# LayerNorm output turned to features by VectorE blocks and SBUF transfers, for seven of eight chunks

## The chip, the cores and the metric

The kernel runs on one NeuronCore of a Trainium2 chip. The metric is the device time of one execution in microseconds. A core has a matrix engine (TensorE, PE in the profile; its weight loads are PEld), three element-wise engines (VectorE or DVE, ScalarE or ACT, GpSimd or POOL) and SyncE (SP), whose queue issues all of this kernel's DMAs. Each engine works through its own instructions in order and waits on semaphores.

## The reference

Two blocks follow each other on x of 2 batches x 2048 tokens x 512 features, all in float32. Cut to what matters:

```python
# block 1: a diagonal complex state space layer (S5) and a feed-forward, conditioned on t
y_mod = _ln(y) * (1 + scale_a) + shift_a
y = y + gate_a * _s5(y_mod, ...)            # a scan along the tokens
y_norm = _ln(y) * (1 + scale_c) + shift_c
y_mod = y_norm * (1 + scale_ff) + shift_ff
y = y + gate_ff * (gelu(y_mod @ W1 + b1) @ W2 + b2)
# block 2: attention, 16 heads of 32, between two conditioned norms
h = gamma * (_ln(hidden) * ln_g + ln_b) + beta
qkv = h @ Wqkv.T + bqkv
att = softmax(q @ k.T) / sqrt(D)
h1 = (att @ v) @ Wp.T + bp + hidden
return gamma * (_ln(h1) * ln_g + ln_b) + beta + h1
```

The scan and the recurrence need the tokens in their order. Attention does not: softmax and the sum over keys are the same for any order of the keys, as long as queries and outputs are put back in their rows.

## The kernel before

The tokens are cut into eight chunks of 512 (`CH`; four per batch), held as 4 tiles of 128 tokens (`TT`) by 512 features, with tokens on the partitions. Every matrix product needs its input the other way round: features on the partitions, as `fT` of 4 quarters (`KC`) of 128 features by 512 tokens. Three norms per chunk are turned like that: the one before S5, the one before the feed-forward and the one before attention.

`normalised` (L392) takes mean and deviation on VectorE and writes `xn`, of which there is one buffer. `features` (L403) then makes one quarter with `to_features` (L145): four TensorE transposes of 128x128 into one PSUM bank (L149), and one ScalarE activation that applies scale and shift and writes `fT` (L150). The banks come from `Banks` (L191): two that take turns, used by all the small products as well.

The loop over chunks (L628) is a schedule written out by hand. One pass does the feed-forward of chunk `now` in 16 steps f: `ff_first` (L484) multiplies by a column block of W1 into `ph` (2 buffers), ScalarE's Gelu makes `hid` (L491, 3 buffers), and `ff_second` (L495) multiplies the `hid` of the step before into `po` (L500). A table `due[f, half]` says which other work is put behind step f: half 0 after `ff_first(f)`, half 1 after `ff_second(f-1)`. In it stand, for the chunk behind, `at_norm` at (0, 1), the four quarters `at_features` from (2, 0) to (3, 1), the eight key and query products `at_heads` (L523) from (4, 1) on, and the four `at_values` from (12, 1) on; for the chunk ahead, `normalised` at (3, 1), the S5 quarters from (5, 0), S5 itself at 7 to 11, `ff_norm` at (12, 0) and the feed-forward quarters from (14, 0). `load_x` of the chunk after that is at (3, 1). Where the batch changes (the pass of chunk 3), `s5_gates` builds three gate rows on TensorE at (3, 0), a fourth row follows at (3, 1), and a fifth after that pass's feed-forward.

`at_norm` (L513) also adds a bias to x on POOL (L517) and stores x to the DRAM buffer `x2` (L518), from which the residual is read after attention. `at_heads` cuts its results into two halves and stores them to DRAM; `at_values` does the same whole. Attention (from about 1400 us) reads keys, queries and values back, block by block, and ends in `close` and `last_close`, which store rows of `out`.

The chunks' x tiles are three buffers in turn, `x0` to `x2`; `fT` has two buffers in turn by chunk, `f0` and `f1`, for S5 and the feed-forward, and one, `hT`, for attention. SP's queue holds the loads and stores in the order of the code.

Of the kernel before, what the change touches and what calls it, by code (L numbers as in the profile page):

```python
# [8 lines left out]
F32 = mybir.dt.float32  # L9
# [4 lines left out]
AF = mybir.ActivationFunctionType  # L14
# [5 lines left out]
P = 128  # L20
# [13 lines left out]
V_D, V_B1, V_B2, V_LNG, V_LNB, V_BQ, V_BK, V_BV, V_BP = 40, 44, 60, 64, 68, 72, 76, 80, 84  # L34
# [5 lines left out]
def tile_s5_block_then_sln_attention(  # L40
# [21 lines left out]
    nc = tc.nc  # L62
    NB, L, D = x.shape
    KC = D // P
    CH = 512
    TT = CH // P
# [12 lines left out]
    vec = const.tile([P, N_VECS], F32, name="vec")  # L79
# [22 lines left out]
    x2 = [dpool.tile([L, D], F32, name=f"x2_{b}") for b in range(NB)]  # L102
# [42 lines left out]
    def to_features(dst, xn, scale, shift, b, k, psum, tag):  # L145

        pt = psum.tile([P, CH], F32, name="pt_tf", tag=tag)
        for t in range(TT):
            nc.tensor.transpose(pt[:, t * P : (t + 1) * P], xn[:, t, k * P : (k + 1) * P], ident)  # L149
        nc.scalar.activation(  # L150
            dst[:, k, :], pt, AF.Identity,
            bias=shift[:, k, b : b + 1], scale=scale[:, k, b : b + 1],
        )
# [23 lines left out]
    xnp = late.enter_context(tc.tile_pool(name="xnp", bufs=1))  # L177
    xlate = late.enter_context(tc.tile_pool(name="xlate", bufs=1))
    wlate = late.enter_context(tc.tile_pool(name="wlate", bufs=1))
# [4 lines left out]
    xpool = early.enter_context(tc.tile_pool(name="xpool", bufs=1, side="right"))  # L184
# [3 lines left out]
    feat = early.enter_context(tc.tile_pool(name="feat", bufs=1, side="right"))  # L188
# [10 lines left out]

    order = [(b, c) for b in range(NB) for c in range(NCH)]  # L200
    index = {bc: i for i, bc in enumerate(order)}
    xt, xns, fts = {}, {}, {}

    def load_x(b, c):
        i = index[b, c] % 3
# [54 lines left out]
    for q in range(4):  # L260
        f = FC // 4
# [67 lines left out]
    t_re = s5c.tile([P, CH], F32, name="t_re")  # L329
    t_im = s5c.tile([P, CH], F32, name="t_im")  # L330
# [54 lines left out]
    gate, last, bus, hs, pos, hids = {}, {}, {}, {}, {}, {}  # L385
# [6 lines left out]
    def normalised(b, c):  # L392

        xc = xt[b, c]
        mean = small.tile([P, TT], F32, name="mean")
        rstd = small.tile([P, TT], F32, name="rstd")
        ln_stats(xc, TT, mean, rstd)
        xn = xnp.tile([P, TT, D], F32, name="xn")
        for t in range(TT):
            normalise(xn[:, t, :], xc[:, t, :], mean, rstd, t)  # L400
        xns[b, c] = xn

    def features(b, c, k, scale, shift, tag):  # L403
        if k == 0:
            fts[b, c] = (wlate if tag == "hT" else feat).tile([P, KC, CH], F32, name="fT", tag=tag)
        to_features(fts[b, c], xns[b, c], scale, shift, b, k, ones, None)

    def tag_of(b, c):
        return f"f{index[b, c] % 2}"
# [15 lines left out]
    def s5_turn(b, c):  # L425

        bu = bus.pop((b, c))
        m = [s5w.tile([P, CH], F32, name=f"m{i}") for i in range(6)]
        nc.vector.tensor_mul(m[0], bu[0], t_re)
        nc.vector.tensor_mul(m[3], bu[0], t_im)  # L430
        nc.vector.tensor_mul(m[1], bu[1], t_im)
        nc.vector.tensor_mul(m[2], bu[1], t_re)  # L432
        nc.vector.tensor_add(m[0], m[0], m[1])
        nc.gpsimd.tensor_tensor(m[2], m[2], m[3], ALU.subtract)  # L434
        bus[b, c] = m
# [48 lines left out]
    def ff_first(b, c, f):  # L484
        ph = ps1.tile([P, CH], F32, name="ph")
        for k in range(KC):
            nc.tensor.matmul(  # L487
                ph, w1_sb[:, k, f * P : (f + 1) * P], fts[b, c][:, k, :], start=k == 0, stop=k == KC - 1
            )
        hids[f] = work1.tile([P, CH], F32, name="hid", bufs=3)  # L490
        nc.scalar.activation(  # L491
            hids[f], ph, AF.Gelu_apprx_tanh, bias=vec[:, V_B1 + f : V_B1 + f + 1], scale=1.0
        )

    def ff_second(b, c, f):  # L495
# [9 lines left out]
    def ff_out(b, c):  # L505
        xc, po = xt[b, c], pos.pop((b, c))
        for t in range(TT):
            g = work1.tile([P, D], F32, name="gated")
            nc.vector.tensor_mul(g, po[:, t, :], gate[b, "gate_f"])  # L509
            nc.gpsimd.tensor_tensor(xc[:, t, :], xc[:, t, :], g, ALU.add)  # L510


    def at_norm(b, c):  # L513
        normalised(b, c)
        xc = xt.pop((b, c))
        for t in range(TT):
            nc.gpsimd.tensor_tensor(xc[:, t, :], xc[:, t, :], bp_row, ALU.add)  # L517
        nc.sync.dma_start(x2[b][c * CH : (c + 1) * CH, :].rearrange("(t p) d -> p t d", p=P), xc)  # L518

    def at_features(b, c, k):  # L520
        features(b, c, k, s_scale, s_shift, "hT")
# [38 lines left out]
    spare = ps1.tile([P, TT, D], F32, name="spare", tag="po", bufs=1)  # L560
# [67 lines left out]
    for i, now in enumerate(order):  # L628

        due = {(f, h): [] for f in range(FC + 1) for h in range(2)}  # L630
        ahead = order[i + 1] if i + 1 < len(order) else None
        behind = order[i - 1] if i else None

        def quarters_from(f, what, chunk):
            for k in range(KC):
                due[f + k // 2, k % 2].append((what, *chunk, k))

        if i == 0:
            due[1, 1].append((rest_of_mod,))
            due[2, 1].append((rows_of_biases,))  # L640
        if behind:
            due[0, 1].append((at_norm, *behind))
            quarters_from(2, at_features, behind)
            for j in range(2 * KC):
                due[4 + j, 1].append((at_heads, *behind, j))
            for t in range(TT):
                if ahead:
                    due[12 + t, 1].append((at_values, *behind, t))
        if ahead:
            if ahead[1] == 0:  # L650
                due[3, 0].append((s5_gates, ahead[0]))
                due[3, 1].append((gate_row, ahead[0], "gb2", gate_b2))
            due[3, 1].append((normalised, *ahead))
            quarters_from(5, s5_features, ahead)
            due[7, 1].append((s5_in, *ahead))
            due[7, 1].append((s5_turn, *ahead))
            due[8, 1].append((s5_scan, *ahead))
            due[8, 1].append((s5_direct, *ahead))
            quarters_from(10, s5_out, ahead)
            due[12, 0].append((ff_norm, *ahead))  # L660
            quarters_from(14, ff_features, ahead)
        if i + 2 < len(order):
            due[3, 1].append((load_x, *order[i + 2]))

        def run_due(at):
            for what, *args in due[at]:
                what(*args)

        for f in range(FC):
            ff_first(*now, f)  # L670
            run_due((f, 0))
            if f:
                ff_second(*now, f - 1)
            run_due((f, 1))
        ff_second(*now, FC - 1)
        ff_out(*now)
        if ahead and ahead[0] != now[0]:
            gate_row(ahead[0], "gate_f", mod[:, GATE_F])
    early.close()
# [190 lines left out]
    def invert(b, c, heads=slice(0, NH), width=64):  # L870
        sm = held.pop((b, c, "sm"))
        nc.vector.reciprocal(sm, sm)
        nc.sync.dma_start(invd[b][heads, c * CH : (c + 1) * CH].rearrange("h (s i) -> h s i", i=width), sm)

    def fetch(b, qt):

        at = slice(qt * P, (qt + 1) * P)
        o4 = work.tile([P, NG, P], F32, name="o4")
        nc.sync.dma_start(o4, od[b][:, at].rearrange("(g r) q -> r g q", r=P))
        by = work.tile([P, NG, P], F32, name="by")  # L880
        heads = invd[b][:, at].rearrange("(g j) q -> j g q", j=4)
        for j in range(4):
            nc.sync.dma_start(
                by[32 * j : 32 * j + 32, :, :], heads[j : j + 1, :, :].to_broadcast([32, NG, P])
            )
        xr = work.tile([P, D], F32, name="xr", bufs=3)
        nc.sync.dma_start(xr, x2[b][at, :])
        held[b, qt] = o4, by, xr
# [66 lines left out]
    def close(b, qt):  # L955

        h, ht, w, mv, y, v = held.pop((b, qt))
        nc.gpsimd.tensor_tensor(ht, w, ht, ALU.add)
        nc.sync.dma_start(out[b, qt * P : (qt + 1) * P, :], ht)


    def deviation(b, qt):
# [14 lines left out]
    def last_close(b, qt):  # L977
        h, y = held.pop((b, qt))
        nc.gpsimd.tensor_tensor(h, h, ending[b][1], ALU.add)
        nc.gpsimd.tensor_tensor(y, y, h, ALU.add)  # L980
        nc.sync.dma_start(out[b, qt * P : (qt + 1) * P, :], y)

# [128 lines left out]
    keeps, m = [], 0  # L1113
# [15 lines left out]
    due = {}  # L1129
# [21 lines left out]
    for b in range(NB):  # L1151
        for c in range(NQ):
            j = NP * (blocks.index((b, NPAIR - 1, c)) + 1) + 1
            if (b, c) == (LB, LC):
                most, rest = slice(0, NH - 4), slice(NH - 4, NH - 2)
                j = NP * (N - 1)
# [22 lines left out]
            for t in range(TT):  # L1179
                qt = c * TT + t  # L1180
                if b == LB:
                    k = j + 3 + 2 * t
# [8 lines left out]
                else:  # L1191

                    k = NP * (NPAIR * NQ * (b + 1) + 2 + 3 * qt // 2)
# [19 lines left out]
    for j in range(FIRST, NP * N + 2):  # L1213
# [18 lines left out]
        n, i = block_at(j + AHEAD)  # L1232
# [91 lines left out]
```

## Time and profile before

| What | Value |
|---|---|
| Time, median of 3 runs | 3458.43 us (3457.08 to 3461.29) |
| The profiled execution | 3459.56 us, span 3457.8 us, granted TensorE clock 0.990 |
| PE busy over the span | 3335.5 us, 96% |
| DVE, ACT, POOL busy | 2151.7, 1939.8, 2137.8 us |
| Chunk stage (to about 1450 us) | one regular pass 170 us |
| TensorE transposes of L149 | 384, of which 336 between 100 and 1400 us |

The chunk stage takes slices 1 to 17 of the profile's 40, attention the rest. A row of a group gives the line, the engine, the operation, what it writes and reads, how often, and after the bar the busy time in us, the mean of one in ns and the engine's idle time before it. A row of the timeline gives the start and the time taken, in us from the span's start, and in brackets the idle time ahead of it and what ended it. TensorE's instructions are pipelined, so one can start before the one ahead has ended: for its cost, take the distance from start to start. "x8" of a product is four matmuls, each in two instructions.

### The profile page before, as it was taken

Reading aid. Unit: us, or ns where it says so; the run is one execution under the profiler, and the core shown is the slowest. Engines: PE = TensorE matmul, PEld = TensorE weight load, DVE = VectorE, ACT = ScalarE, POOL = GpSimd, SP = SyncE. Lnnn points to the kernel's source line nnn. Section 1 sums busy time; section 2 is a strip of 40 time slices with the busy share of each in tenths; the row PEclk is TensorE's granted clock in tenths of the full one; section 3 lists DMA queues with packets and bytes.
Section 4 is the critical chain, followed back from the end, with each engine's and each line's share of the span. In section 5 each row is a group of like instructions: output and inputs, shape, how many; then the busy total and the mean of one; then the engine's idle time right before and its main releaser. Section 6 shows DMA issues by size and latency. Waiting matters only on the chain.

```text
span 3457.8 us, 34348 instructions
## 1 busy us (share of the span) xinstructions
PE 3335.5 (96%) x11764; PEld 1508.3 (44%) x11764; DVE 2151.7 (62%) x2976; ACT 1939.8 (56%) x2208; POOL 2137.8 (62%) x1162
## 2 busy tenths in 40 slices
PE   7999999999999999999999999999999999999997
PEld 4444444444444444444444444444444444444432
DVE  6232323232322310688888888888888888888885
ACT  2111111111111111398999999999888888888963
POOL 4133131313131310289898989998898989899986
PEclk8999999999999999999999999999999999999999
DMA  8001111111110112432223222223234233233233
GB/s 304 1 31 43 43 43 43 43 43 43 43 43 31 43 37 61 121 77 67 58 62 72 66 67 54 72 67 75 70 81 96 65 87 85 71 85 78 61 97 115
DMA packets 201396, 237.06 MB, mean 69 GB/s; under 512 B 89544, under 2 KB 118728, under 8 KB 197126
## 3 DMA queue, kind: packets, MB, share of 16 engines
q1 hardware_dynamic: 201222, 234.87, 24.5%
q8 instruction: 93, 1.52, 0.2%
q14 instruction: 81, 0.66, 0.1%
HBM read 166.77 MB, written 67.76 MB: 68 GB/s over the span
## 4 chain that ended last, share of the span: by engine, by line
PE 73%; DVE 14%; ACT 8%; issue 2%; DMA 1%; POOL 1%; SPq 0%; DVEq 0%; ACTq 0%; POOLq 0%
PE o L834 15%; PE ph L487 13%; PE po L500 13%; PE s L754 10%; DVE run L770 10%; PE pk L530 6%; ACT x L765 4%; PE pv L542 3%; PE m L779 3%; PE py L905 2%; PE pt_run L790 2%; ACT pT L824 2%; ACT x L824 2%; PE pu L421 2%; PE pt_tf L149 1%
## 5 line engine op out<-in xcount | busy, mean ns | idle before, releaser
L813 POOL TENSOR_TENSOR x<-x,shift 128x1024 f32<-128x1024 f32 x704 | 1653.8, 2387 | 153.6 <-DMA shift<-flat 104.6
L765 ACT COPY x<-s 128x1024 f32<-128x1024 f32 x704 | 692.4, 1012 | 213.0 <-PE s L754 211.9
L770 DVE TENSOR_TENSOR run<-s,run 128x1024 f32<-128x1024 f32 x576 | 702.9, 1220 | 73.6 <-ACT x L765 50.2
L824 ACT ACTIVATE x<-x 128x1024 f32<-128x1024 f32 x704 | 739.8, 1060 | 11.9 <-POOL x L813 11.6
L754 PE MATMUL s<-qs,ks 128*128 128x512 f32 x2048 | 669.5, 421 | 51.3 <-DVE run L770 45.2
L834 PE MATMUL o<-x,v 128*64 128x512 f32 x2816 | 718.4, 612 | 0.0
L487 PE MATMUL ph<-fT,w_sb 128*128 128x512 f32 x1024 | 463.5, 597 | 0.0
L500 PE MATMUL po<-w_sb,hid 128*128 128x512 f32 x1024 | 460.3, 592 | 0.0
L754 PEld LDWEIGHTS s<-qs,ks 128*128 128x128 f32 x2048 | 334.4, 189 | 275.4 <-DVE run L770 149.7
L819 DVE TENSOR_TENSOR pT<-s,shift 128x1024 f32<-128x1024 f32 x320 | 389.5, 1217 | 85.1 <-PE s L754 85.1
L784 DVE TENSOR_REDUCE top<-m 128x1 f32<-128x640 f32 x512 | 417.4, 815 | 9.8 <-PE m L779 7.1
L491 ACT ACTIVATE hid<-ph,vec 128x512 f32<-128x512 f32 x128 | 88.0, 687 | 595.9 <-PE ph L487 595.9
L824 ACT ACTIVATE pT<-pT 128x1024 f32<-128x1024 f32 x320 | 339.4, 1061 | 50.2 <-DVE pT L819 50.2
L158 DVE SCALAR_TENSOR_TENSOR lo<-pk,vec,hi 128x512 fp32r<-128x512 f32 x64 | 48.0, 751 | 494.4 <-ACT hi L157 494.4
L834 PE MATMUL o<-pT,v 128*64 128x512 f32 x1280 | 330.5, 595 | 7.9 <-ACT pT L824 7.9
L487 PEld LDWEIGHTS ph<-fT,w_sb 128*128 128x128 f32 x1024 | 193.3, 192 | 228.9 <-issue 228.9
L834 PEld LDWEIGHTS o<-x,v 128*64 128x64 f32 x2816 | 157.1, 135 | 310.4 <-issue 191.4
L434 POOL TENSOR_TENSOR m<-m,m 128x512 f32<-128x512 f32 x8 | 13.1, 1643 | 449.7 <-DVE m L432 449.7
L500 PEld LDWEIGHTS po<-w_sb,hid 128*128 128x128 f32 x1024 | 190.7, 190 | 221.5 <-issue 221.5
L779 PE MATMUL m<-ks,qs 128*128 128x320 f32 x1024 | 256.6, 332 | 17.3 <-DVE top L784 15.5
L157 ACT ACTIVATE hi<-pk,vec 128x512 fp32r<-128x512 f32 x64 | 44.0, 687 | 383.3 <-PE pk L530 383.3
L510 POOL TENSOR_TENSOR x<-x,gated 128x512 f32<-128x512 f32 x32 | 39.6, 1269 | 354.4 <-DVE gated L509 354.4
(253 smaller groups left out, 2774.6 us busy)
## 6 DMA issues: line engine op xcount, KB each, us to landing
ks<-kd SPq DMA_DIRECT2D x128, 256.0 KB
qs<-qd SPq DMA_DIRECT2D x512, 64.0 KB
shift<-flat SPq DMA_DIRECT2D x64, 512.0 KB
x<-in_x SPq DMA_DIRECT2D x8, 1024.0 KB
w_sb<-in_w SPq DMA_DIRECT2D x8, 1024.0 KB
x<-x SPq DMA_DIRECT2D x8, 1024.0 KB
kd<-hi SPq DMA_DIRECT2D x32, 256.0 KB
kd<-lo SPq DMA_DIRECT2D x32, 256.0 KB
```

What stands on the lines that cost most here:

```text
L487: nc.tensor.matmul(ph, w1_sb[:, k, f * P : (f + 1) * P], fts[b, c][:, k, :], start=k == 0, stop=k == KC - 1)
L500: nc.tensor.matmul(pos[b, c][:, t, :], hid[:, t * P : (t + 1) * P], w2_sb[:, f, :], start=f == 0, stop=f == FC - 1,)
L530: nc.tensor.matmul(pk, w[:, k, g * P : (g + 1) * P], hT[:, k, :], start=k == 0, stop=k == KC - 1)
L754: nc.tensor.matmul(s[:, e, :], kst[pair_of[n], e][:, kt * P : (kt + 1) * P], qst[n][:, e, :], start=True, stop=True,)
L765: nc.scalar.copy(x, s)
L770: nc.vector.tensor_tensor(runs[n], s, kept[n, 0] if kt == 1 else runs[n], ALU.max)
L779: nc.tensor.matmul(m[:, i, :YW], qst[n][:, e, t * P : (t + 1) * P], kst[pair_of[n], e][:, k : k + YW], start=True, stop=True,)
L784: nc.vector.tensor_reduce(tops[n][:, j, 0:1], m[:, :, :YW], AX.XY, ALU.max, negate=True)
L813: nc.gpsimd.tensor_tensor(x, x, shifts[n], ALU.add)
L819: nc.vector.tensor_tensor(x, s, shifts[n], ALU.add)
L824: nc.scalar.activation(x, x, AF.Exp)
L834: nc.tensor.matmul(outs[n][64 * e : 64 * e + 64, :], v[:, kt, e : e + 2, :], x[:, e, :], start=first, stop=final,)
```

## The change

For seven chunks at each of the three norms, the transposes on TensorE are replaced. The tables of which chunk goes which way are in `blocked`: chunk 0's S5 and feed-forward norms and the last chunk's attention norm keep the old way.

`by_blocks` turns each of the four token tiles with one VectorE transpose, which turns every 32x32 block where it stands. Then 16 transfers inside SBUF, issued on SP, bring each block row to the partitions where its features belong: 32 partitions with four runs of 512 bytes each, 64 KB a transfer. ScalarE's activation reads the moved quarter from SBUF instead of a PSUM bank. For the attention and feed-forward norms, `fT` itself holds the turned blocks and the moved data lands in the buffer of `xn`; for the S5 norm `xn` is still needed, so the turned blocks stand in the x tile of the chunk that will be loaded next (`s5_blocks`), the moved data in `fT`, and that chunk's `load_x` goes from (3, 1) to (7, 0).

The tokens of such a chunk come out in another order: token t*128 + a*32 + j stands at place a*128 + t*32 + j. The S5 products and the Gelu put them back in time order by reading and writing in runs of 32. Attention leaves them in the new order; the store to `x2` follows it with four DMAs in place of one, and `store` writes the rows of `out` to where they belong. For the last chunk both stay as they were.

```diff
     def features(b, c, k, scale, shift, tag):
+        if (b, c) in blocked:
+            nc.scalar.activation(
+                fts[b, c][:, k, :], blocked[b, c][:, k, :], AF.Identity,
+                bias=shift[:, k, b : b + 1], scale=scale[:, k, b : b + 1],
+            )
+            return
...
+    def by_blocks(b, c, tag, spare=None):
+        xn = xns[b, c]
+        fts[b, c] = fT = (wlate if tag == "hT" else feat).tile([P, KC, CH], F32, name="fT", tag=tag)
+        turned = (fT if spare is None else spare).rearrange("p k (g t j) -> p (k g) t j", g=4, j=32)
+        for t in range(TT):
+            nc.vector.transpose(turned[:, :, t, :], xn[:, t, :].rearrange("p (f j) -> p f j", j=32))
+        moved = xnp.tile([P, KC, CH], F32, name="moved", tag="xn") if spare is None else fT
+        turned = (fT if spare is None else spare).rearrange("p k (g x) -> p k g x", g=4)
+        for a in range(4):
+            for g in range(4):
+                nc.sync.dma_start(
+                    moved[32 * g : 32 * g + 32, :, a * P : (a + 1) * P], turned[32 * a : 32 * a + 32, :, g, :]
+                )
+        blocked[b, c] = moved
+
+    def s5_blocks(b, c, i):
+        spare = (xlate if i == 1 else xpool).tile([P, KC, CH], F32, name="turned", tag=f"x{i}")
+        by_blocks(b, c, tag_of(b, c), spare)
...
-        nc.vector.tensor_mul(m[0], bu[0], t_re)
...
+        for i, j, t in ((0, 0, t_re), (3, 0, t_im), (1, 1, t_im), (2, 1, t_re)):
+            nc.vector.tensor_mul(in_time(m[i], b, c), as_made(bu[j], b, c), in_time(t, b, c))
...
-            hids[f], ph, AF.Gelu_apprx_tanh, bias=vec[:, V_B1 + f : V_B1 + f + 1], scale=1.0
+            in_time(hids[f], b, c), as_made(ph, b, c), AF.Gelu_apprx_tanh, bias=vec[:, V_B1 + f : V_B1 + f + 1], scale=1.0
...
-        nc.sync.dma_start(x2[b][c * CH : (c + 1) * CH, :].rearrange("(t p) d -> p t d", p=P), xc)
...
+        rows = rows.rearrange("(a t j) d -> a j t d", t=TT, j=32)
+        for a in range(4):
+            nc.sync.dma_start(rows[a], xc[32 * a : 32 * a + 32, :, :])
...
             due[0, 1].append((at_norm, *behind))
+            due[0, 1].append((by_blocks, *behind, "hT"))
...
             due[3, 1].append((normalised, *ahead))
+            due[3, 1].append((s5_blocks, *ahead, (i + 2) % 3))
...
             due[12, 0].append((ff_norm, *ahead))
+            due[12, 0].append((by_blocks, *ahead, tag_of(*ahead)))
...
-            due[3, 1].append((load_x, *order[i + 2]))
+            due[7, 0].append((load_x, *order[i + 2]))
```

`in_time` and `as_made` only view a tile's 512 tokens in runs of 32, by place and by time. `store` replaces the output DMA in `close` and `last_close` and changes the rows it writes to.

More of the change, by code (lines that the diff above doesn't have):

```diff
@@ L201, in tile_s5_block_then_sln_attention @@
     index = {bc: i for i, bc in enumerate(order)}
-    xt, xns, fts = {}, {}, {}
+    xt, xns, fts, blocked = {}, {}, {}, {}
     def load_x(b, c):
@@ L397, in normalised @@
         ln_stats(xc, TT, mean, rstd)
-        xn = xnp.tile([P, TT, D], F32, name="xn")
+        xn = xnp.tile([P, TT, D], F32, name="xn", tag="xn")
         for t in range(TT):
@@ L406, in features, with in_time, as_made @@
         to_features(fts[b, c], xns[b, c], scale, shift, b, k, ones, None)
+    def by_blocks(b, c, tag, spare=None):
[15 more added lines that the diff above has]
+        by_blocks(b, c, tag_of(b, c), spare)
+    def in_time(ap, b, c):
+        return ap.rearrange("p (t a j) -> p a t j", a=4, j=32) if (b, c) in blocked else ap
+    def as_made(ap, b, c):
+        return ap.rearrange("p (a t j) -> p a t j", a=4, j=32) if (b, c) in blocked else ap
     def tag_of(b, c):
@@ L428, in s5_turn @@
         m = [s5w.tile([P, CH], F32, name=f"m{i}") for i in range(6)]
-        nc.vector.tensor_mul(m[0], bu[0], t_re)
-        nc.vector.tensor_mul(m[3], bu[0], t_im)
-        nc.vector.tensor_mul(m[1], bu[1], t_im)
-        nc.vector.tensor_mul(m[2], bu[1], t_re)
+        for i, j, t in ((0, 0, t_re), (3, 0, t_im), (1, 1, t_im), (2, 1, t_re)):
+            nc.vector.tensor_mul(in_time(m[i], b, c), as_made(bu[j], b, c), in_time(t, b, c))
         nc.vector.tensor_add(m[0], m[0], m[1])
@@ L517, in at_norm @@
             nc.gpsimd.tensor_tensor(xc[:, t, :], xc[:, t, :], bp_row, ALU.add)
-        nc.sync.dma_start(x2[b][c * CH : (c + 1) * CH, :].rearrange("(t p) d -> p t d", p=P), xc)
+        rows = x2[b][c * CH : (c + 1) * CH, :]
+        if (b, c) == order[-1]:
+            nc.sync.dma_start(rows.rearrange("(t p) d -> p t d", p=P), xc)
+            return
+        rows = rows.rearrange("(a t j) d -> a j t d", t=TT, j=32)
+        for a in range(4):
+            nc.sync.dma_start(rows[a], xc[32 * a : 32 * a + 32, :, :])
     def at_features(b, c, k):
@@ L676, in tile_s5_block_then_sln_attention @@
         ff_out(*now)
+        blocked.pop(now, None)
         if ahead and ahead[0] != now[0]:
@@ L873, in invert, with store @@
         nc.sync.dma_start(invd[b][heads, c * CH : (c + 1) * CH].rearrange("h (s i) -> h s i", i=width), sm)
+    def store(b, qt, rows):
+        c, a = divmod(qt, TT)
+        if (b, c) == order[-1]:
+            nc.sync.dma_start(out[b, qt * P : (qt + 1) * P, :], rows)
+        else:
+            to = out[b, c * CH : (c + 1) * CH, :].rearrange("(t a j) d -> a t j d", a=4, j=32)[a]
+            nc.sync.dma_start(to, rows)
     def fetch(b, qt):
@@ L958, in close @@
         nc.gpsimd.tensor_tensor(ht, w, ht, ALU.add)
-        nc.sync.dma_start(out[b, qt * P : (qt + 1) * P, :], ht)
+        store(b, qt, ht)
     def deviation(b, qt):
@@ L980, in last_close @@
         nc.gpsimd.tensor_tensor(y, y, h, ALU.add)
-        nc.sync.dma_start(out[b, qt * P : (qt + 1) * P, :], y)
+        store(b, qt, y)
     LB, LC = NB - 1, NQ - 1
```

## The prediction

> **What bounds the kernel now.** I read the page's 40 slices first.
>
> ```profile
> PE   7999999999999999999999999999999999999997
> ACT  2111111111111111398999999999888888888963
> PEclk8999999999999999999999999999999999999999
> ```
>
> The change sits in slices 1 to 17 (the eight chunks, to about 1450 us). TensorE is full there at full clock, ScalarE almost idle. Part 1 gives VectorE 62% over the span, but nearly all of that is the attention after slice 17. Then the groups kept apart by shape, from 100 to 1400 us, and the busy times of one regular pass:
>
> ```profile
> L149 PE MATMUL pt_tf<-ident,xn 128*128 128x128 f32 x336 | 50.4, 273 | 0.0
> L150 ACT ACTIVATE fT<-pt_tf,s_shift,s_scale 128x512 f32<-128x512 f32 x28 | 21.7, 774 | 40.9 <-PE pt_tf L149 40.9
> ...
> 390.00:560.00 170.00, 170.00 (x433) 77.64 (x432) 49.11 (x104) 24.95 (x36) 43.21 (x32) 1.00 0.13 44
> ```
>
> The first row holds exactly the transposes that the change removes, and none waited. The last row reads PE, PEld, DVE, ACT, POOL: in a 170 us pass PE works all 170, VectorE 49, ScalarE 25, DMA has a 0.13 share. So time taken off PE here comes off the run, unless PE starts to wait. Where it could wait shows in the timeline of that pass (chunk 2's feed-forward, with chunk 1's attention projections inside it):
>
> ```profile
> 403.83 0.60 PE L149 MATMUL pt_tf<-ident,xn 128*128 128x128 f32 x4
> 404.26 3.60 PE L500 MATMUL po<-w_sb,hid 128*128 128x512 f32 x8
> ...
> 419.32 3.60 PE L500 MATMUL po<-w_sb,hid 128*128 128x512 f32 x8
> ...
> 411.83 0.69 ACT L491 ACTIVATE hid<-ph,vec 128x512 f32<-128x512 f32 x1 [2.72 <-PE ph L487]
> ...
> 400.38 5.48 POOL L517 TENSOR_TENSOR x<-x,bp_row 128x512 f32<-128x512 f32 x4 [4.37 <-DVE xn L141]
> ...
> 405.89 0.37 SPq L518 DMA_DIRECT2D x<-x  x1
> ...
> 399.69 3.81 DVE L141 TENSOR_SCALAR xn<-x,mean,rstd 128x512 f32<-128x512 f32 x4
> ```
>
> Four transposes hold PE from 403.83 to 404.26. The Gelu of f=3 (411.83) has 7 us in hand before its matmuls at 419.32. Last, the SP queue's own rows, for the price of an issue:
>
> ```profile
> 2436.88 1.93 SPq L883 DMA_DIRECT2D by<-invd  x4
> 3397.96 4.26 SPq L1013 DMA_DIRECT2D w<-wp  x4
> ```
>
> `by` moves 32 partitions of four 512-byte runs, the shape of the new transfers: 1.93/4 = 0.48 us an issue. `w` is the only SBUF to SBUF transfer in this kernel.
>
> [...] the trace has 273 ns as duration, but 0.109 us from start to start, and only the latter is saved. [...] 691 ns at 512, as L509's 0.69 here; no VectorE transpose stands in the trace. [...] here the semaphores of the four `w` show 2.7 to 4.3 us from issue to landing, and the 1 MB store L518 took 4.4. [...] 3.81 us for four beside POOL's L517, 1.91 alone.
>
> **The change, part by part.** The program's order has 336 PE transposes fewer (7 chunks x 3 norms x 16), 84 VectorE transposes more and 357 more DMAs on SP (336 moves, and seven stores L518 cut in four). ScalarE has the same count.
>
> *Removed.* 84 groups of four at 0.435 us: **36.6 us** of PE, all on the path.
>
> *Moves for the attention norm* (seven passes, chunks 0 to 6). Before, PE turned a quarter just before ScalarE needed it. Now ScalarE's first quarter waits for all 16 moves, and behind it in its queue stand the second quarter and the Gelu of f=3. In the pass above:
> - VectorE normalises until 403.5; four transposes at 0.69 (estimate[...]) end by 406.3. They cost no more than that even at 1.1 us each, since SP is not free before 407.8.
> - SP: the store waits for POOL's L517, until 405.9, and is four issues now, 4 x 0.48: 407.8. Then 16 moves at 0.48; the last is issued at 407.8 + 15 x 0.48 = 415.0.
> - Landing: 2.0 us after issue at best, 4.3 at worst (`w`). I take 2.9, as 1 MB of stores goes out beside the first moves: **417.9**.
> - ScalarE: two quarters from SBUF at 0.6, Gelu 0.69, handoffs 0.2: 420.0.
> - PE without four groups of transposes is at the matmuls of f=3 at 419.32 - 4 x 0.435 = 417.6. Wait: **2.4 us**.
>
> Five passes are like this one. The pass of chunk 4 starts with 0.9 us of row broadcast on PE while the chain already runs (its store leaves 14.9 us after the first `ph`, here 15.8): 1.5 us. The pass of chunk 3 builds batch 1's gate rows: three `pt_ar` groups on two PSUM banks, the third waiting for ScalarE's copy of the first, which now stands behind both quarters, the Gelu and a third quarter. That copy ends 3.1 us after landing, 30.9 us into the pass, where PE asks at 22.4: 8.6 us, after which the Gelu is no longer late. Sum: 5 x 2.4 + 1.5 + 8.6 = **22.1 us** given back.
>
> *Moves for the S5 norm.* VectorE's normalise waits for ScalarE's fourth quarter (xn's buffer holds the moved chunk): about 421.2; then 1.9 + 2.8 + 16 x 0.48 + 2.9, landing at 436. What stands behind on ScalarE is the Gelu of f=6, which PE reads at about 451. Slack 12 us: nothing. On SP the key stores wait behind the moves till 434; their double buffers are asked for at 447. The buffer lent for the turned data was stored to DRAM by 412, long before VectorE writes it at 423.
>
> *Moves for the feed-forward norm.* No store stands before them; two to three f lie between the norm and its first quarter and the end of the pass behind that. Before, in the pass of chunk 3, normalise ended at 698.1: turned by 701, landed by 712, when the first quarter was due. Slack until the Gelu of f=15 about 15 us: nothing. VectorE's evacuation of `pv` waits 2.8 us behind the transposes; the other bank serves PE.
>
> *Load of x.* SP issues it at f=7 instead of f=3 and it lands in 5 us; its reader comes a pass later. The moves before it have landed by then, so SP does not stand.
>
> *The rest.* 84 x 0.69 = 58 us of VectorE spread over passes where it idles 121 of 170 us; Gelu and the S5 products in permuted runs of 32 floats keep their element count (doubled, the Gelu would add 0.7 a pass, 5 us; a quarter cheaper gains 1 us); the output stores keep rows of 2 KB. Attention works on permuted tokens with the same instructions: nothing.
>
> Sum: the profiled execution is 3459.56 us (span 3457.8 and 1.8 around it), 1.1 over the median 3458.43. 3459.6 - 36.6 + 22.1 = 3445.1; against the median, **3444**.
>
> **The rivals.** Each microsecond of landing time counts seven times, so all turns on the moves' pace.
> - *The moves come in time.* At 0.35 us an issue (the quickest `by` took 0.30) and 2.0 us of landing they are in by 414.7, the Gelu is ready at 416.8, and only the gate pass waits, 5.4 us: 3427. For it: 2 MB in 10 us is within what the DMA engines move (304 GB/s in slice 0). Against: no row of four such issues ran at that pace.
> - *ScalarE's wait outweighs the transposes: slower.* The place is the same, the first attention quarter before the Gelu of f=3; the price is seven times the lateness; it decides from a landing at 420.0, that is from 0.62 us a move. At 0.8 us: landing 422.7, 22.1 + 7 x 4.8 = 55.7 us given back, 3478. For it: the four `by` land 1.3 to 1.8 us apart, and SP holds eight DMA semaphores, so a move cannot be issued before the eighth ahead of it has landed; over 3.8 us of landing that sets the pace. Against: `by` reads one DRAM row 32 times; the 512-byte packets of the trace take 27 ns at the median, 128 of them on 16 engines 0.22 us.
> - *No transposes leave PE's path.* Not possible: the program's order has them gone.
>
> **How the numbers follow.** In time 0.13; late by less than the transposes (3430 to 3451) 0.49; about even 0.12; slower 0.26. A measurement tells about 0.2%, 7 us, from no change, so faster 0.62, same 0.12, slower 0.26. The range goes from the first rival (3427, less 3 for a gate pass that hides) to 0.8 us a move: 3424 to 3480. The cases that are faster hold 3424 to 3451.
>
> **What would show it.** Right: no `pt_tf` between 100 and 1380 us; in each pass ScalarE's first attention quarter starts some 28 us in, released by a DMA, and PE idles 2 to 3 us before `po` of f=3, 8 us before the third gate row; waits of PE in this part of about 22 us; the S5 and feed-forward quarters cost PE nothing. Wrong: SP more than 0.6 us a move, or PE waiting at f=6 or f=15, or passes longer by VectorE's lateness.

## The result: 1.2% slower, and the profile after

| Kernel | Median, us | Ratio to before, 95% interval |
|---|---|---|
| before | 3459.86 (3457.08 to 3465.84, 4 runs) | |
| after | 3501.03 (3499.96 to 3502.42, 4 runs) | 1.0118 [1.0103, 1.0133] |

The prediction was 3444 us, in a range of 3424 to 3480. The kernel became slower, and by more than the range allowed. The profiled execution after has a span of 3500.6 us, 42.8 more than before, at a granted clock of 0.982 where it was 0.990.

The 40 slices after, the two rows of TensorE:

```profile
PE   7999998999999999999999999999999999999987
...
PEclk8999999999999999999999999999999999999998
```

They look nearly as before; TensorE still seems full. The regular pass says more. The stretch of 170 us below has, as columns, TensorE, weight loads, VectorE, ScalarE and GpSimd, then the clock and the share of the DMA engines:

```profile
393.00:563.00 170.00, 163.70 (x377) 72.13 (x376) 53.99 (x113) 24.82 (x36) 40.49 (x30) 0.98 0.22 62
```

TensorE, which worked all 170 us before, is idle for 6.3, its clock is below 1.00, and it issues 377 instructions in the stretch instead of 433. A whole pass, from the first `ph` of one to that of the next, went from 170.1 us to 173.3 to 174.2; the pass of chunk 3, which builds the gate rows, from 175.0 to 184.0. TensorE's waits (in all, times, longest):

```profile
PE po L536 <- ACT hid L527: 37.4, 6, 6.5
PE o L880 <- ACT pT L870: 16.7, 5, 5.7
...
PE pt_ar L164 <- ACT r_scale L168: 12.8, 1, 12.8
```

The first and the third are new: six waits for the Gelu of f=3 and one for ScalarE's copy of a gate row, 50.2 us together. The second was 7.9 us before; it lies in the last 100 us of attention. The timeline of the pass that the prediction worked through:

```profile
405.17 2.87 SPq L560 DMA_DIRECT2D x<-x  x4
...
408.15 11.27 SPq L429 DMA_DIRECT2D moved<-fT  x16
...
402.70 2.48 DVE L424 STREAM_TRANSPOSE fT<-xn 128x512 f32<-128x512 f32 x4
...
413.31 3.60 PE L523 MATMUL ph<-fT,w_sb 128*128 128x512 f32 x8
...
421.07 1.52 ACT L405 ACTIVATE fT<-moved,s_shift,s_scale 128x512 f32<-128x512 f32 x2 [17.10 <-DMA moved<-fT]
422.49 0.67 ACT L527 ACTIVATE hid<-ph,vec 128x512 f32<-128x512 f32 x1
...
423.21 5.90 PE L536 MATMUL po<-w_sb,hid 128*128 128x512 f32 x8 [6.30 <-ACT hid L527]
```

The reader sees the chain that was predicted, with other sizes: four VectorE transposes take 2.48 us, four stores and 16 moves follow on SP, the moves hold it for 11.27 us, ScalarE stands until the last has landed, two quarters and the Gelu follow, and TensorE has waited 6.30 us. The last row holds one thing more: the same eight instructions that take 3.60 us elsewhere take 5.90 after the wait.

### The profile page after: what moved, and what is told of

Read it like the earlier page. It is cut to its first block, busy times and chain, and to the rows that moved or that the text cites. A ratio compares the mean times of both kernels' runs of the same rounds, so it can differ in the third digit from the quotient of the medians.

```text
span 3500.6 us, 34317 instructions
## 1 busy us (share of the span) xinstructions
PE 3321.4 (95%) x11428; PEld 1483.5 (42%) x11428; DVE 2199.7 (63%) x3060; ACT 1939.7 (55%) x2208; POOL 2138.6 (61%) x1162
## 4 chain that ended last, share of the span: by engine, by line
PE 66%; DVE 14%; ACT 9%; DMA 3%; SPq 3%; issue 3%; POOL 2%; DVEq 0%; ACTq 0%; POOLq 0%
PE o L880 15%; PE po L536 11%; PE s L800 10%; PE ph L523 9%; DVE run L816 9%; PE pk L572 6%; ACT x L811 4%; PE pv L584 3%; PE m L825 3%; PE py L960 2%; SPq L429 2%; PE pt_run L836 2%; ACT x L870 2%; ACT pT L870 2%; PE pu L459 2%
## 5 line engine op out<-in xcount | busy, mean ns | idle before, releaser
L536 PE MATMUL po<-w_sb,hid 128*128 128x512 f32 x1024 | 476.6, 610 | 37.4 <-ACT hid L527 37.4
L880 PE MATMUL o<-pT,v 128*64 128x512 f32 x1280 | 330.8, 595 | 16.7 <-ACT pT L870 16.7
L536 PEld LDWEIGHTS po<-w_sb,hid 128*128 128x128 f32 x1024 | 200.2, 196 | 293.6 <-issue 251.2
```

What stands on the lines that cost most here:

```text
L536: nc.tensor.matmul(pos[b, c][:, t, :], hid[:, t * P : (t + 1) * P], w2_sb[:, f, :], start=f == 0, stop=f == FC - 1,)
L880: nc.tensor.matmul(outs[n][64 * e : 64 * e + 64, :], v[:, kt, e : e + 2, :], x[:, e, :], start=first, stop=final,)
```

## The experiments

All ratios are to the kernel before, run on the same chip beside them (medians 3459.18 us for experiments 1, 2, 3 and 5, 3457.2 for 4, 6, 7 and 8). Where a text says how far TensorE is ahead or behind, its instructions in attention, the same in all kernels, are laid beside those of the kernel before. The tail is what that one does from 3340 us on.

**1. The S5 and feed-forward norms alone (e2_s5_ff_only).** Attention's norm keeps the old way, so its moves, the permuted tokens and both changed stores go.

```diff
-            due[0, 1].append((by_blocks, *behind, "hT"))
...
-        if (b, c) == order[-1]:
+        if True:
             nc.sync.dma_start(rows.rearrange("(t p) d -> p t d", p=P), xc)
...
-        if (b, c) == order[-1]:
+        if True:
             nc.sync.dma_start(out[b, qt * P : (qt + 1) * P, :], rows)
```

> The changed kernel with attention's norm turned by TensorE as before (112 transposes stay there), and with it the plain stores to x2 and to the output; S5's and the feed-forward's norms go by blocks. Theory (only attention's moves are late; S5's and the feed-forward's have slack): no PE wait in the chunk stage beyond the kernel before's, 224 x 0.109 = 24.4 us saved: 3435, ratio 0.993. Rival (the moves cost PE something at S5 and the feed-forward as well, or VectorE's 56 transposes delay it): ratio 0.997 or above, with PE waits at f=6 or f=15.

Measured: 3436.64 us, 0.9933 [0.9917, 0.995]. A regular pass takes 166.6 us, 3.5 less than before, which is eight groups of four transposes at 0.435 us. No wait for `hid` or for a gate row is left in TensorE's list, and the tail's wait is as it was:

```profile
PE o L879 <- ACT pT L869: 7.4, 5, 2.2
```

So nearly all of the loss comes from attention's norm: its moves in the pass, and its order of tokens at the end. The other two norms bring the whole of what they take off TensorE, which is 25.5 us ahead as the chunk stage ends. Of these, 4.7 are lost again later, in slow matmuls of the kind that experiment 3 shows.

**2. Quarters later (e4_quarters_later).** The moves stay; attention's quarters go from step 2 to step 3, its heads one step later, and the gate rows ahead of them.

```diff
-            quarters_from(2, at_features, behind)
+            for k in range(KC):
+                due[3, k // 2].append((at_features, *behind, k))
...
-                due[4 + j, 1].append((at_heads, *behind, j))
+                due[5 + j, 1].append((at_heads, *behind, j))
...
-                due[3, 0].append((s5_gates, ahead[0]))
+                due[1, 0].append((s5_gates, ahead[0]))
```

> The changed kernel with the place of ScalarE's work alone moved: attention's four quarters stand behind the Gelu of f=3 (two at each half of step 3) instead of f=2, the key and query products start one step later, chunk 3's gate rows are built at step 1. Stores and moves are as in the changed kernel. Theory (the loss is the Gelu of f=3 and the gate copies standing behind a wait for the moves, and the half clock that follows): PE waits about 1 us a pass for the Gelu of f=4, no half clock between 104 and 1480 us, 36.6 - 7 saved and 11 lost at the end: 3441, ratio 0.9945. Rival (the moves themselves slow PE, or the wait only goes to the next place): waits of 3 us and more at f=4 or at the first key product, 3470 or above.

Measured: 3438.72 us, 0.9942 [0.9928, 0.9957]. TensorE's waits for the Gelu:

```profile
PE po L536 <- ACT hid L527: 4.5, 5, 1.1
```

The gate rows' wait is gone, and the clock is 1.00 over the pass. The moves still take 11.27 us in the same pass (401.15 us on); nothing urgent stands behind them in ScalarE's queue any more. Some 62 us come back with the same transfers, by the place of ScalarE's work alone: 45.7 us of waits, and the slow matmuls behind them.

**3. Moves ahead of the stores (e3_moves_first).** `at_norm` issues the 16 moves before the four stores to `x2`, so that SP need not wait for GpSimd's `x`.

```diff
+        by_blocks(b, c, "hT")
         rows = rows.rearrange("(a t j) d -> a j t d", t=TT, j=32)
...
-            due[0, 1].append((by_blocks, *behind, "hT"))
```

> The changed kernel with SP's order turned round in the attention norm: the 16 moves first, then the four stores to x2. Theory (the moves land one issue of 0.64 us after the other, and start late because four stores stand before them and slow the first two): moves start at the end of VectorE's transposes, 2.9 us earlier, the first two take 0.6 instead of 1.1 us; landing 3.9 us earlier, PE waits 2.5 us instead of 6.5 in six passes and 9 instead of 12.9 in chunk 3's: 27 us back, 3474. If the half clock after each wait needs a wait of more than 2.5 us, six times some 2.7 us more: 3458. Rival (DMA engines, not SP's issues, set the pace): landing unchanged, 3500.

Measured: 3462.86 us (20 runs), 1.001 [1.0003, 1.0017]. This lies between the two values expected. In the profile the moves start at 400.24, with no store in flight, and take 10.24 us; the waits fall to 22.4 us (13.9 for `hid`, 8.5 for the gate row). Three rows of the timeline, with nearly the same wait ahead of the first two:

```profile
414.24 3.70 PE L536 MATMUL po<-w_sb,hid 128*128 128x512 f32 x8 [2.33 <-ACT hid L527]
...
927.91 5.32 PE L536 MATMUL po<-w_sb,hid 128*128 128x512 f32 x8 [2.32 <-ACT hid L527]
...
1266.17 3.70 PE L536 MATMUL po<-w_sb,hid 128*128 128x512 f32 x8 [2.37 <-ACT hid L527]
```

The second is slow, the other two are not. TensorE's clock explains it. In the traces it reads either 1.00 or 0.50, and its changes stand on a grid of 3.41 us: every spell of half clock that ends within the run lasts 3.41 us or a multiple (in the kernel after 3.41, 6.83, 10.24 or 13.65). Here are the grid's steps around the second wait and around the third, with TensorE's busy time first and the clock third from the end:

```profile
924.38:927.79 3.41, 1.21 (x3) 0.19 (x1) 0.00 (x0) 2.02 (x4) 0.00 (x0) 1.00 0.81 173
927.79:931.20 3.41, 3.29 (x4) 1.51 (x5) 1.90 (x5) 2.05 (x4) 0.00 (x0) 0.50 0.59 164
...
1262.29:1265.70 3.41, 1.51 (x4) 0.38 (x2) 0.00 (x0) 1.67 (x3) 0.00 (x0) 1.00 0.81 168
1265.70:1269.11 3.41, 2.94 (x7) 1.44 (x8) 0.00 (x0) 2.40 (x4) 0.00 (x0) 1.00 0.72 183
```

A step with 1.21 us of work is followed by one at half clock, a step with 1.51 us is not. So it goes in all ten traces (140 to 1380 us, the chunk stage): after each of the 31 steps at full clock with at most 1.43 us of work the clock was halved, and after none with 1.51 us or more. So the extra length of those eight instructions goes with the clock, not with the data, and the length of a wait alone does not decide it. Waits of 2.32, 2.44 and 3.01 us were followed by it, waits of 1.39, 2.33 and 2.37 were not, and in the kernel after all seven, of 5.6 us and more, were. The grid lies differently in the executions profiled (one of its steps begins 2.77 us after the start here, 1.01 in the kernel after, 1.71 in the kernel before), so whether a wait of this length costs more than itself is luck. Of the 20 runs the quickest, with 3455 us, has the highest granted clock, 0.989; the others have 0.985 to 0.987.

**4. Both (e8_later_first).** The edits of experiments 2 and 3 together:

```diff
+        by_blocks(b, c, "hT")
         rows = rows.rearrange("(a t j) d -> a j t d", t=TT, j=32)
...
+                due[3, k // 2].append((at_features, *behind, k))
...
+                due[5 + j, 1].append((at_heads, *behind, j))
...
+                due[1, 0].append((s5_gates, ahead[0]))
```

> The two edits together that keep ScalarE's wait from PE: moves ahead of the stores, and the four quarters behind the Gelu of f=3. The output stores stay as in the changed kernel. Theory: the 1 us waits at f=4 go as well, PE has no wait in the chunk stage; 36.6 saved, 11 lost at the end: 3434, ratio 0.9925. Rival (no more than the quarters alone): 3439.

Measured: 3431.2 us, 0.992 [0.9904, 0.9937]. A regular pass takes 164.8 us: 170.1 before, less twelve groups at 0.435. One stretch of the chunk stage:

```profile
390.00:560.00 170.00, 170.00 (x415) 76.85 (x414) 61.48 (x123) 26.56 (x39) 48.28 (x36) 1.00 0.22 62
```

TensorE is full again at full clock, with 61 us of VectorE and 0.22 of the DMA engines beside it. The change's idea pays there in full. TensorE is 39.9 us ahead of the kernel before where the tail begins, but only 28.8 at its end: the tail still loses 11.1.

**5. The output in four stores (e1_store_in_four).** In `store`, each block of 32 rows gets a DMA of its own. Its bytes are the same.

```diff
-            to = out[b, c * CH : (c + 1) * CH, :].rearrange("(t a j) d -> a t j d", a=4, j=32)[a]
-            nc.sync.dma_start(to, rows)
+            for t in range(TT):
+                at = c * CH + t * P + a * 32
+                nc.sync.dma_start(out[b, at : at + 32, :], rows[32 * t : 32 * t + 32, :])
```

> The changed kernel with one edit: each output store of a permuted 128-row tile is cut in four stores of 32 partitions, each to 32 rows that lie together, in place of one store whose rows go in 4 x 32. Theory (the store with a leading dimension of 4 [...] lands after 15 us instead of 2, and the last tiles' only y buffer waits for it): output stores land in 2 to 3 us, VectorE's waits for them go back to 3 to 5 us, PE's waits for pT in the last 100 us fall from 16.7 to about 8 us, and 11 us come back: 3490, ratio to the kernel before 1.0088. Rival (the last 100 us are slower because the shifted chunk stage brings transfers together otherwise): stays at 3500, ratio 1.0118.

Measured: 3503.57 us, 1.0127 [1.0112, 1.0142]. That missed: no gain. By the semaphores, the stores of `y` land 7.0 us (median) after issue in the kernel after, 2.2 before and 1.7 here, so the late landing was real and is cured. The 15 us that were expected were a misreading: such a store updates its semaphore five times, not sixteen, and the fifth update is its landing. VectorE's wait to write `y` (one buffer) again; first after, then this kernel:

```profile
DVE y L1029 <- DMA out<-y: 29.4, 5, 9.5
```

```profile
DVE y L1030 <- DMA out<-y: 21.7, 4, 7.7
```

Before it was 14.2. TensorE's wait for `pT` fell from 16.7 to 12.2 us. Set beside the kernel after, the tail gives back 5.2 us (6.4 behind, then 1.2), but 5.3 had been lost in the middle of attention, and 1.1 before it. The first piece, some 3 us, is lost here:

```profile
2572.51 3.93 SPq L929 DMA_DIRECT2D out<-xr  x4
...
2578.43 3.07 SPq L939 DMA_DIRECT2D by<-invd  x4
...
2587.52 1.28 POOL L948 TENSOR_TENSOR o<-o,by 128x512 f32<-128x512 f32 x1 [2.14 <-DMA by<-invd]
...
2588.76 4.70 POOL L859 TENSOR_TENSOR x<-x,shift 128x1024 f32<-128x1024 f32 x2
...
2591.17 1.06 ACT L870 ACTIVATE x<-x 128x1024 f32<-128x1024 f32 x1 [2.14 <-POOL x L859]
```

Four stores take SP for 3.93 us, where the one store in the kernel after took 0.57; the load of `by` comes late by that, GpSimd waits 2.14 us for it, and ScalarE as long for GpSimd. TensorE then waits 1.71 us, and the four `py` matmuls after it take 3.51 us, 1.88 in the kernel after. A gain at the end was paid for in the middle.

**6. Four stores for the last batch only (e9_and_four_last).** The edits of experiment 4, and the four stores where the tail is.

```diff
             to = out[b, c * CH : (c + 1) * CH, :].rearrange("(t a j) d -> a t j d", a=4, j=32)[a]
+            if b == NB - 1:
+                for t in range(TT):
+                    nc.sync.dma_start(to[t], rows[32 * t : 32 * t + 32, :])
+                return
             nc.sync.dma_start(to, rows)
```

> The run with both edits, and in addition the output stores of the last batch alone in four pieces of 32 rows (the first batch keeps its single slow store, so that SP has no more issues in the middle of attention). Theory (cutting all 28 gained 5 us at the end and lost as much in the middle, where SP's four issues delay the next tile's fetches): the end gains 5 to 6 us, the middle loses nothing: 3428, ratio 0.991. Rival (the end's loss is not the stores' at all): as the run without it, 3434.

Measured: 3428.92 us, 0.9917 [0.9902, 0.9932]: the fastest of all, 28 us under before on this chip, but not to be told from experiment 4 by time (2.3 us, and the intervals overlap). In the traces the tail loses 6.7 us (38.6 ahead, then 31.9) instead of 11.1, with VectorE's wait for `y` at 18.9 us. In experiment 1, where attention isn't permuted, the tail lost 2.9.

**7. Half of attention's moves from ScalarE's queue (e5_half_on_act).** The second eight moves are issued by ScalarE just before its first quarter.

```diff
+        if tag == "hT":
+            move(nc.sync, (0, 1))
+            halves_due[b, c] = lambda: move(nc.scalar, (2, 3))
+        else:
+            move(nc.sync, range(4))
...
+            if k == 0 and (b, c) in halves_due:
+                halves_due.pop((b, c))()
```

> The changed kernel with half of the attention norm's 16 moves issued from ScalarE's queue, just ahead of its first quarter, where it would stand waiting anyway; the other eight stay on SP behind the four stores. Theory (SP's issues, 0.64 us each and one after the other, set the landing; the DMA engines have room): SP's last move goes out 5.1 us earlier, ScalarE's eight are out by 410.5 on the scale of the pass that starts at 389.3; landing 5 us earlier, PE waits 1.3 us instead of 6.5 in six passes and about 8 instead of 12.9 in chunk 3's, no half clock in the six: 3501 - 6 x 8 - 5 = 3448, ratio 0.997. Rival (data rate or landing time sets it): the moves of both queues land one after the other as before, 3500.

Measured: 3476.95 us, 1.0054 [1.0039, 1.0069]: better than after, but far from what was expected.

```profile
402.28 3.47 SPq L569 DMA_DIRECT2D x<-x  x4
402.41 7.88 ACTq L432 DMA_DIRECT2D moved<-fT  x8
...
408.74 5.11 SPq L432 DMA_DIRECT2D moved<-fT  x8
...
417.57 3.70 PE L545 MATMUL po<-w_sb,hid 128*128 128x512 f32 x8 [3.55 <-ACT hid L536]
```

The two queues didn't share the time. ScalarE's eight took 7.88 us beside the 1 MB of stores (0.6 to 1.56 us each). SP had issued its stores by 405.75, yet its first move left at 408.74: it waited for a DMA semaphore whose last user was ScalarE's third move, landed at 408.66. This kernel hands out eight such semaphores over both queues; in the traces of the kernels before and after, with eight on SP, no transfer was issued before the one eight ahead of it had landed. The last move landed 28.9 us into the pass instead of 31.6.

The wait shown, 3.55 us, left the clock whole: it fell on two steps of the grid, and each had more than 1.5 us of work in it. The six others in this trace, of 2.82 us and more, were followed by half clock.

```profile
412.29:415.70 3.41, 1.73 (x5) 0.42 (x3) 0.00 (x0) 0.27 (x1) 0.00 (x0) 1.00 0.33 78
415.71:419.12 3.41, 1.55 (x4) 0.83 (x5) 0.16 (x1) 3.41 (x6) 0.00 (x0) 1.00 0.00 0
```

**8. Attention's moves in halves (e10_half_moves).** Each move becomes two of 32 KB: twice the transfers, the same bytes.

```diff
-                nc.sync.dma_start(
-                    moved[32 * g : 32 * g + 32, :, a * P : (a + 1) * P], turned[32 * a : 32 * a + 32, :, g, :]
-                )
+                for ks in (range(KC),) if tag != "hT" else (range(2), range(2, 4)):
+                    ks = slice(ks[0], ks[-1] + 1)
+                    nc.sync.dma_start(
+                        moved[32 * g : 32 * g + 32, ks, a * P : (a + 1) * P], turned[32 * a : 32 * a + 32, ks, g, :]
+                    )
```

> The changed kernel with each of the attention norm's moves cut in two of half the runs (32 transfers of 32 KB for 16 of 64 KB, the same bytes). Theory (an SBUF to SBUF transfer costs SP about 0.6 us whatever it carries): the moves take SP 20 us instead of 10.3, landing 10 us later, seven times: about 3571. Rival (the issue is priced by its runs): SP's time for the moves and the run's time stay as they are, 3501.

Measured: 3567.42 us, 1.0316 [1.0296, 1.0337], as expected.

```profile
418.00 21.84 SPq L431 DMA_DIRECT2D moved<-fT  x32
```

```profile
PE po L538 <- ACT hid L529: 93.5, 6, 15.9
...
PE pt_ar L164 <- ACT r_scale L168: 22.2, 1, 22.2
```

The second fence shows TensorE's waits. Sixteen transfers more, at half the size, hold SP 10.6 us longer, 0.66 each: the price is that of a transfer, not of its bytes or runs. (The 32 partitions were the same in both.)

## Why the prediction was wrong

**Right.** The 336 transposes left TensorE's path and are worth 36.6 us (experiments 1 and 4: 3.5 and 5.3 us a pass). The place of the new wait, f=3 and the third gate row, was right, and so was what stands behind it in ScalarE's queue. The S5 and feed-forward moves cost TensorE nothing, as argued (experiment 1). VectorE's four transposes take 2.48 us, against an estimate of 2.76, four times the 0.69 that VectorE's L509 takes for 128x512 in the trace of before. The Gelu in runs of 32 takes 685 ns, 687 before.

**The step that failed first: 0.48 us an issue.** It was taken from `by`, which reads DRAM. In the chain of waits after, every move has its own row:

```profile
406.01 0.69 SPq L560
...
406.75 1.29 SPq L560
...
408.15 1.12 SPq L429
...
409.31 1.10 SPq L429
...
410.45 0.60 SPq L429
...
418.18 0.60 SPq L429
...
418.82 2.02 DMA moved<-fT
```

Fourteen moves leave 0.64 us apart, the first two 1.1 behind the stores. This is how the lateness adds up, in us from the first `ph` of the pass:

| Step | Predicted | Measured |
|---|---|---|
| four stores to `x2` issued | 17.7 | 18.8 |
| last move issued | 24.9 | 29.5 |
| landed | 27.8 | 31.6 |
| `hid` ready: two quarters and the Gelu | 29.9 | 33.9 |
| TensorE asks for it | 27.5 | 27.6 |
| wait | 2.4 | 6.3 |

The landing itself was quicker (2.0 us, 2.9 predicted); nearly all else is issue. With 3.8 us more at each of seven places, 22.1 becomes 48.7, and 50.2 were measured; the gate row's 12.8 against 8.6 is the same shift. In other words the prediction's own rival, ScalarE's wait outweighing the transposes, came true: it decides from 0.62 us a move, and the sixteen took 11.27 us, 0.70 each. The nearer row was in the prediction: `w`, the kernel's only transfer inside SBUF, with 4.26 us for four. Its own issues, 0.51 to 0.61 us in the trace of before, were not read out; DRAM's row was taken since its shape of runs was the same, and experiment 8 shows that the runs don't set the price.

By itself this would have ended near 3472 us, inside the range. **Two terms were missing altogether**, and either of them, added to that, leads out of it.

*The matmuls after a wait.* TensorE is 30.5 us behind where the chunk stage ends: -36.6 for the transposes, +50.2 for the waits, and some 17 that no wait accounts for. The group after the wait shows where they are: 5.90 us instead of 3.60. The steps of the clock's grid there:

```profile
417.44:420.85 3.41, 0.00 (x0) 0.00 (x0) 0.00 (x0) 0.00 (x0) 0.00 (x0) 1.00 0.40 96
420.85:424.26 3.41, 1.05 (x2) 0.54 (x3) 0.00 (x0) 3.19 (x5) 0.00 (x0) 0.50 0.00 0
424.26:427.67 3.41, 3.41 (x6) 1.34 (x5) 3.07 (x7) 0.88 (x2) 0.00 (x0) 0.50 0.00 0
427.67:431.09 3.42, 3.42 (x9) 1.51 (x8) 1.24 (x3) 0.00 (x0) 0.00 (x0) 1.00 0.12 30
```

A whole step is idle, two at half clock follow, and in these TensorE works for 4.46 us, of which it loses half. After the seven waits it works 34.2 us at half clock: 17.1 us lost, 1.7 to 3.0 a wait. That is the missing part. In the traces the step ahead of half clock was not always idle: with up to 1.43 us of work in it the clock was halved as well (experiment 3). The prediction priced only a wait's length. At its own 2.4 us each wait would have been a toss for 1.7 us more, half of one 3.41 us step: an estimate from experiment 3, where half clock followed waits of 2.32 and 2.44 us and not those of 2.33 and 2.37.

*The end of attention.* TensorE falls from 30.2 to 42.6 us behind in the tail. It is idle there for 7.9 us more than before, almost all in its waits for `pT`, and it works 13.0 us at half clock instead of 3.4, which loses 4.8 us more. The prediction said that the output stores keep rows of 2 KB and cost nothing. Rows weren't what mattered: `store` writes four groups of 32 rows in one DMA, and such a store's semaphore has one update 1.0 us after issue and four from 5.1 us on, where the store before has sixteen, from 1.8 us on. It lands after 7.0 us, against 2.2 before for the same bytes and 1.7 in rows of 32 (experiment 5); why so late was not shown. `y` has one buffer, and its next writer stands for it, here for 9.53 us, most of it after the store's issue:

```profile
3440.15 0.63 SPq L928 DMA_DIRECT2D out<-y  x1
...
3447.43 0.69 DVE L1029 TENSOR_TENSOR y<-z,g_row 128x512 f32<-128x512 f32 x1 [9.53 <-DMA out<-y]
...
3452.57 1.97 PE L880 MATMUL o<-pT,v 128*64 128x512 f32 x4 [5.70 <-ACT pT L870]
3454.47 5.79 PE L960 MATMUL py<-wp,o 128*128 128x512 f32 x8
```

Behind `y` on VectorE stands work for `pT`, which ScalarE and TensorE want; the last two rows, 1.08 and 3.70 us before, show the half clock after the wait. Shown is that quicker landings give back 5.2 us of the tail in experiment 5 and 4.4 in experiment 6. Of the 7.2 and 6.7 us that the tail still loses there, 2.9 and 2.7 are half clock, the rest longer waits for `pT`; what makes these longer is open. In experiment 1 the tail's 2.9 us are half clock alone.

The sum: -36.6 + 50.2 + 17.1 + 12.4 = 43.1 us, against 42.8 between the two spans.

## What to carry to other kernels

Work taken off the bound engine and put into a chain of transfers pays only if nothing urgent stands behind the chain's end in a queue: here the same moves gave 1.2% slower or 0.8% faster (experiment 4), depending on where ScalarE's four quarters and SP's four stores stood. Price an issue from a row with the same source and destination memories (0.64 us from start to start inside SBUF here, 0.48 in the row that read DRAM), count 16 issues as 16 prices, and add the slow matmuls to the longer waits of the matrix engine: in the chunk stage here waits of 2.3 to 3.6 us cost them or not by their place on the clock's grid, and all from 3.64 us on did. When a store is cut differently, read how long it takes to land and who writes its buffer next, then what its extra issues push back in the same queue.

## What was not expected of the hardware

- A transfer of 32 or 64 KB inside SBUF costs SP 0.60 us and 0.64 from start to start; right behind 1 MB of stores the first two took 1.1 each on SP, and in the pass shown up to 1.56 on ScalarE's queue.
- TensorE's clock was halved after each step of a 3.41 us grid with at most 1.43 us of work in it, and after none with 1.51 us or more (chunk stage, ten traces). So waits of 2.32 and 2.44 us lost it and one of 3.55 us did not. In the kernel after, a fall cost 1.7 to 3.0 us.
- One store of 256 KB with four groups of 32 rows landed after 7.0 us, four of 64 KB after 1.7 each.
- ScalarE's quarter takes 802 ns from SBUF, against 774 from PSUM before; the prediction had 0.6 us, its author's estimate, but successive quarters start 0.71 apart.
